# A selective scan re-tiled: eight channels by sixteen states on the partitions, sums in column quadrants, delta spread by DMA

## The chip, the cores and the metric

The kernel runs on one core of a Trainium2 chip. The metric is the device time in microseconds (us) of one execution. Times named below come from the timed runs or from one profiled execution of the kernel before.

## The reference, cut to what matters

A two-layer decoder works on 64 sequences of 128 tokens with 128 features. Layer 0 is a cumulative-sum attention, a cross-attention, and a mixture of experts (two shared ones and eight routed ones, of which each token uses two). Layer 1 is a selective scan, a second cross-attention and a quantised feed-forward part; each of these six blocks ends in a residual and a layer norm. The change is in layer 1's scan and in where the experts of layer 0 are run. The scan has 256 channels `e` and 16 states `n`:

```python
def step(h, inp):
    d_t, u_t, b_t, c_t = inp
    dA = jnp.exp(d_t[..., None] * A)                      # (b, e, n)
    h = dA * h + (d_t * u_t)[..., None] * b_t[:, None, :]
    y = jnp.einsum('ben,bn->be', h, c_t)                  # sum over the states
    return (h, y)
# delta = softplus(dt @ dt_proj_w + dt_bias), A = -exp(A_log); y + u * D follows
```

The experts of layer 0, over the tokens `xf`:

```python
acc = acc + cw[:, None] * ((silu(xf @ e1.T) * (xf @ e3.T)) @ e2.T)   # for 8 routed experts; 2 shared ones have no cw
```

## The kernel before, in words

**Groups.** The 64 sequences are worked in 16 groups `g` of four (`G`), so a row of 512 elements (`W`) holds four sequences of 128 tokens. All is float32 but for the last feed-forward part.

**Order.** Generators (`scan_inputs`, `spread`, `decays`, `states`, `outputs`, `attend`, `feed`, `c_experts` and others) yield steps with an engine, a cost, the keys they depend on and the buffer slots they take. `Flow.run` plays them: it always takes the step with the earliest planned start, shifted by the step's and the thread's `ahead`; a group may start only if it is within `depth` of the oldest unfinished one. A transfer is planned at 0.1 us of the queue and 4.0 us until it lands (`LANDING`). The order that comes out is fixed: each engine then runs its instructions one after the other and waits on semaphores. All transfers are issued on SP's queue.

**Two stages.** Layer 0 runs the first two blocks for all groups, and the experts of the first `EARLY` = 8 groups with weights that stay in memory (`wall`). Layer 1 runs everything else: the experts of the other eight groups with weights streamed in (`streamed`, tile `we`, 384 KB each, ten per group), and the scan, the second cross-attention and the feed-forward part of all groups. An expert group is the lines L302 to L420: hidden products L367, SiLU L384, gate L393, back projection L405, weighting L420.

**The scan.** Channels lie on the partitions, 128 at a time (`c` = 0, 1), and a step `(c, n)` handles two states, so a group has 16 steps and every tile of a step is 128 x 1024. `scan_inputs` computes delta, du = delta * u and the projection that holds B and C; it writes the projection's 48 rows to DRAM (`rows`, L1071). `spread` reads for each step two rows of B and two of C back, broadcast to all 128 partitions (L1154, 512 KB each). `decays` makes dA = exp(A * delta) on ACT, 127 of each 128 tokens, the first being zeroed once so that the scan restarts (L1169). `states` multiplies du with B into PSUM (`bu`, L1185) and runs the scan along the free axis (`h`, L1193), both on DVE. `outputs` multiplies by C on POOL (L1217); that product is held behind the next step's L1185. TensorE then adds the states of the step to `acc` with an identity matrix as weights (L1230):

```python
def add(acc):
    for j in range(2):
        mm(acc, ident, HS[g, c, n][:, j, :], start=n + j == 0, stop=n + j == NS - 1)
```

After the 16 states, L1241 adds u * D. A float32 matmul shows as two records on TensorE, each with its weight load. Other lines that the text names: L825, layer 0's attention-weighted values, 32 output columns per head group; L1475, the output projection of the second cross-attention; L1068, an eviction of the projection; `mid`, the activations that pass from layer 0 to layer 1 through DRAM.

Of the kernel before, what the change touches and what calls it, by code (L numbers as in the profile page):

```python
# [9 lines left out]
BF16 = mybir.dt.bfloat16  # L10
# [6 lines left out]
P = 128  # L17
B = 64
# [11 lines left out]
EARLY = 8  # L30
# [145 lines left out]
def decoder(ctx: ExitStack, tc: tile.TileContext, t: dict, out: bass.AP):  # L176
# [58 lines left out]
    A_log = reserve("A_log", [P, 2, NS])  # L235
# [221 lines left out]
    with (  # L457
# [404 lines left out]
        def resident(g, e):  # L862
# [6 lines left out]
            behind=lambda g: [("lnA", max(0, 2 * g - 2 + 1), 0)] + ([("c", g - 1, "p", 9, 1)] if g else []),  # L869
# [6 lines left out]
        for g in range(EARLY):  # L876
            flow.add(2 * g, c_route(g, S), c_experts(g, S))
# [8 lines left out]
    with (  # L886
# [7 lines left out]
        negA = new(pc, [P, 2, NS], "negA")  # L894
        act(negA, A_log, AF.Exp)
        dve.tensor_scalar(negA, negA, -1.0, None, ALU.mult)

# [14 lines left out]
        missing = new(p, [3, 3, 256], "B0")  # L912
# [17 lines left out]
        for c in range(8):  # L930
            bvb = new(p, [P, P], f"xq{c % 2}")
            dve.tensor_copy(bvb, ybv[:, c : c + 1].to_broadcast([P, P]))
            mm(pbo, bvb, yWo[:, c, :], start=False, stop=c == 7)
# [39 lines left out]
        sl_xT = slots(2, p, [P, W], "xT")  # L973
# [3 lines left out]
        sl_rows = slots(2, pd, [3 * NS, W], "rows")  # L977
        sl_delta = slots(2, p, [P, 2, W], "delta")
        sl_du = slots(2, p, [P, 2, W], "du")
        sl_B = slots(2, p, [P, 2, W], "B")  # L980
        sl_C = slots(2, p, [P, 2, W], "C")
        sl_dA = Slots([new(p, [P, 2, G, P], f"dA{i}") for i in range(3)])
# [13 lines left out]
        sl_xqb = slots(1, p, [P, G, P], "xqb", BF16)  # L996
# [4 lines left out]


        for dA in sl_dA:
            pool.memset(dA.tile[:, :, :, 0:1], 0.0)

# [9 lines left out]
        def scan_inputs(g):  # L1015
# [45 lines left out]
            def project(pj, _):  # L1061
# [8 lines left out]
            (rows_bc,) = yield SP(  # L1070
                k + ("rows",), [k + ("proj",)], lambda o: nc.sync.dma_start(out=o, in_=proj.tile[0 : 3 * NS, :]), sl_rows  # L1071
            )
            rows_bc.until = ("C", g, 1, NS - 2)

# [19 lines left out]
            proj.until = [k + ("dt", 1), k + ("rows",)]  # L1094
            e.until = k + ("e1",)
            delta.until = ("dA", g, 1, NS - 2)
            e = e.tile
            yield ACT(1.1, k + ("exp",), [], lambda: act(e, e, AF.Exp, scale=-1.0), table="exp")
            du.until = ("B", g, 1, NS - 2)
# [9 lines left out]
            yield POOL(2.0, k + ("du",), [], lambda: pool.tensor_tensor(e1, delta.tile, u.tile, ALU.mult), port=True)  # L1109
            IN[g] = u.tile, delta.tile, e1, rows_bc.tile  # L1110
# [30 lines left out]
        def last(g, kind):  # L1141
            return [(kind, g - 1, 1, NS - 2)] if g else []
# [3 lines left out]
        def spread(g):  # L1146

            yield Wait([("in", g, "rows"), ("in", g, "du")] + last(g, "Cin"))
            for c, n in steps:
                for name, sl, row in (("B", sl_B, NS + n), ("C", sl_C, 2 * NS + n)):  # L1150

                    def fetch(o):
                        src = IN[g][3][row : row + 2, :].rearrange("n s -> (n s)").unsqueeze(0)
                        nc.sync.dma_start(  # L1154
                            out=o.rearrange("p n s -> p (n s)"), in_=src.to_broadcast([P, 2 * W])
                        )

                    (o,) = yield SP((name + "in", g, c, n), [("in", g, "rows"), ("in", g, "du")], fetch, sl)
                    o.until = (name, g, c, n)
                    BC[name, g, c, n] = o.tile  # L1160

        def decays(g):
            yield Wait([("in", g, "du")] + last(g, "dA"))
            delta = IN[g][1].rearrange("p c (b s) -> p c b s", b=G)
            for c, n in steps:

                def exps(dA):
                    for j in range(2):
                        act(  # L1169
                            dA[:, j, :, 1:], delta[:, c, :, 1:], AF.Exp, scale=negA[:, c, n + j : n + j + 1]  # L1170
                        )

                (dA,) = yield ACT(1.4, ("dA", g, c, n), [("in", g, "delta")], exps, sl_dA, table="exp")
                dA.until = ("S", g, c, n)
                DA[g, c, n] = dA.tile
# [3 lines left out]
        def states(g):  # L1179
            yield Wait([("in", g, "du")] + last(g, "S"))  # L1180
            for c, n in steps:

                def first(bu):
                    du = IN[g][2]
                    order[g, c, n] = dve.tensor_tensor(  # L1185
                        bu, du[:, c, :].unsqueeze(1).to_broadcast([P, 2, W]), BC["B", g, c, n], ALU.mult
                    )

                (bu,) = yield DVE(1.25, ("B", g, c, n), [("Bin", g, c, n), ("in", g, "du")], first, sl_bu, ahead=AHEAD, port=True)
                bu.until = ("S", g, c, n)  # L1190

                def scan(h):
                    dve.tensor_tensor_scan(  # L1193
                        h.rearrange("p n s -> p (n s)"), DA[g, c, n].rearrange("p n b s -> p (n b s)"),
                        bu.tile.rearrange("p n s -> p (n s)"), 0.0, ALU.mult, ALU.add,
                    )

                (h,) = yield DVE(2.3, ("S", g, c, n), [("dA", g, c, n)], scan, sl_h, ahead=AHEAD)
                h.until = ("acc", g, c, n)
                HS[g, c, n] = h.tile  # L1200
# [7 lines left out]
        def outputs(g):  # L1208
            yield Wait([("in", g, "du")])
            acc = None  # L1210
            for i, (c, n) in enumerate(steps):
# [3 lines left out]
                def product():  # L1215
                    h = HS[g, c, n]
                    one = pool.tensor_tensor(h, h, BC["C", g, c, n], ALU.mult)  # L1217


                    if behind:  # L1220
                        tc.add_manual_dep(one.ins, order[behind].ins.name, BEHIND, reason="shared reads")

                deps = [("S", g, c, n), ("Cin", g, c, n)]
# [3 lines left out]

                def add(acc):
                    for j in range(2):
                        mm(acc, ident, HS[g, c, n][:, j, :], start=n + j == 0, stop=n + j == NS - 1)  # L1230

                if n == 0:
                    (acc,) = yield PE(1.9, ("acc", g, c, n), [("C", g, c, n)], add, sl_acc)
                    acc.until = ("D", g, c)
                else:
                    yield PE(1.9, ("acc", g, c, n), [("C", g, c, n)], lambda: add(acc.tile))
# [275 lines left out]
        def feed(g):  # L1512
# [17 lines left out]
            def rounded(xq):  # L1530
# [8 lines left out]
                lambda o: dve.tensor_scalar(o.rearrange("p b s -> p (b s)"), xq.tile, MAGIC, None, ALU.subtract), sl_xqb,  # L1539
# [90 lines left out]
        def spaced(g):  # L1630

            at = 2 * (g - EARLY)
            return ([("S", at - 1, 1, 0)] if at else []) + ([("c", g - 1, "mix", 9)] if g > EARLY else [])

# [4 lines left out]
        for g in range(EARLY, NG):  # L1639
            flow.add(min(2 * (g - EARLY), g - 1), c_route(g, S), c_experts(g, S))  # L1640
        for g in range(NG):
            flow.add(g, scan_inputs(g), ahead=0.0)
            flow.add(g, gates(g), residual(g), ahead=0.0)
            flow.add(g, spread(g), decays(g), states(g), ahead=-0.5)
            flow.add(g, outputs(g), ahead=0.0)
            flow.add(g, cross_inputs(g), values(g), ahead=-0.5)
            flow.add(g, *(attend(g, b) for b in range(G)), cross_end(g), ahead=0.0)
            flow.add(g, feed(g), ahead=0.0)
        with tc.manual_schedule():
            flow.run(5)  # L1650


def _laid_out(i):
# [18 lines left out]
    def experts(shared, routed, f):  # L1672
# [37 lines left out]
        "A_log": chunks(i[s + "A_log"]),  # L1710
# [35 lines left out]
```

## Time and profile before

| | |
|---|---|
| time, median of 3 runs | 3479.39 us (3478.55 to 3480.17) |
| profiled execution | 3482.17 us, span 3480.5 us, mean granted clock 0.951 |
| layer 0 ends, first scan product, last scan product (start) | 1044, 1111, 3328 us |
| state sum on TensorE, L1230 | 1024 records, 514.4 us |
| moved by DMA | 353.28 MB, mean 102 GB/s |
| B and C broadcasts | 256 + 256 transfers of 512 KB, 4.8 and 4.0 us from issue to landing |
| expert weights streamed, `we` | 80 transfers of 384 KB, 4.4 us |

A line of the groups reads: source line, engine, operation, output tile <- input tiles, shapes, count | busy us in all, mean ns of one | idle time of the engine just before, and what ended it. PE is TensorE's matmul side, PEld its weight loads, DVE is VectorE, ACT ScalarE, POOL GpSimd, SP the engine that issues transfers. Stretches are given in us from the start of the span.

### The profile page before, as it was taken

What the parts mean: (1) busy time and instruction counts of PE and PEld (TensorE: products, weight loads), DVE (VectorE), ACT (ScalarE), POOL (GpSimd) and SP (SyncE); (2) the same over time, 40 slices, a digit from 0 to 9 for tenths busy, and PEclk for the clock granted to TensorE, in tenths of its full rate; (3) what the DMA queues carried; (4) which work ended last, traced back from release to release, by engine and by line L of the source; (5) the groups of instructions that cost most, each with busy time, mean ns of one, the idle gap of its engine ahead of it and who ended that gap; (6) DMA issues with size and microseconds to landing.
All of it is one profiled execution on the core that took longest, in us unless ns stands there. A gap on an engine that the chain in (4) does not pass through costs nothing.

```text
span 3480.5 us, 56211 instructions
## 1 busy us (share of the span) xinstructions
PE 3136.8 (90%) x20760; PEld 2040.5 (59%) x20760; DVE 2731.1 (78%) x5398; ACT 2182.1 (63%) x3739; POOL 1481.3 (43%) x1222
## 2 busy tenths in 40 slices
PE   4999999999987799989988989989998998999974
PEld 2776766766664465645655556656566555566643
DVE  5867787778754788888789888978879888987963
ACT  3656556665544576766666766767676676767743
POOL 4423433433211554544544454355364544534431
PEclk8999999999998899999999999999999999999976
DMA  2001010010004545354333643433434452442310
GB/s 88 25 7 30 24 27 11 24 30 19 10 10 155 180 150 184 128 179 151 127 116 114 205 142 119 145 136 133 156 132 135 141 173 97 154 166 75 107 46 7
DMA packets 141994, 353.28 MB, mean 102 GB/s; under 512 B 31483, under 2 KB 53654, under 8 KB 141590
## 3 DMA queue, kind: packets, MB, share of 16 engines
q1 hardware_dynamic: 141718, 349.68, 30.2%
q8 instruction: 163, 2.67, 0.3%
q14 instruction: 113, 0.93, 0.1%
HBM read 335.47 MB, written 14.16 MB: 100 GB/s over the span
## 4 chain that ended last, share of the span: by engine, by line
PE 61%; DVE 16%; POOL 6%; DMA 5%; ACT 4%; issue 3%; SPq 0%; DVEq 0%; POOLq 0%; ACTq 0%
PE mm L367 13%; PE acc L1230 7%; PE mm L405 7%; POOL h L1217 3%; DVE h L1193 3%; PE mm L802 3%; PE mm L825 3%; PE mm L1040 3%; PE mm L1446 3%; PE mm L1426 3%; PE mm L1376 2%; DMA we<-in_we 2%; DVE bu L1185 2%; PE mm L1475 2%; PE mm L759 2%
## 5 line engine op out<-in xcount | busy, mean ns | idle before, releaser
L1217 POOL TENSOR_TENSOR h<-h,C 128x1024 f32<-128x1024 f32 x256 | 610.3, 2384 | 709.2 <-DVE bu L1185 410.8
L1193 DVE TENSOR_TENSOR_SCAN h<-dA,bu 128x1024 f32<-128x1024 f32 x256 | 584.5, 2283 | 47.6 <-PE acc L1230 29.4
L1230 PE MATMUL acc<-h,ident 128*128 128x512 f32 x1024 | 514.4, 628 | 72.5 <-POOL h L1217 71.9
L1169 ACT ACTIVATE dA<-delta,negA 128x508 f32<-128x508 f32 x512 | 335.4, 713 | 60.3 <-DVE h L1193 52.7
L1185 DVE TENSOR_TENSOR bu<-du,B 128x1024 f32<-128x1024 f32 x256 | 334.0, 1305 | 27.7 <-DMA B<-rows 25.7
L1230 PEld LDWEIGHTS acc<-h,ident 128*128 128x128 f32 x1024 | 186.0, 197 | 287.4 <-issue 159.3
L367 PE MATMUL mm<-cT,we 128*128 128x512 f32 x640 | 315.1, 611 | 29.7 <-DMA we<-in_we 24.0
L367 PE MATMUL mm<-cT,wall 128*128 128x512 f32 x640 | 303.3, 598 | 0.0
L1419 POOL TENSOR_TENSOR s<-s,rs 128x1232 f32<-128x1232 f32 x64 | 148.6, 2321 | 246.5 <-DVE rs L1413 173.2
L785 POOL TENSOR_TENSOR s<-s,mx 128x1232 f32<-128x1232 f32 x64 | 143.9, 2248 | 215.9 <-DVE mx L782 181.3
L384 ACT ACTIVATE a<-mm 128x512 f32<-128x512 f32 x160 | 94.2, 597 | 179.0 <-PE mm L367 169.4
L367 PEld LDWEIGHTS mm<-cT,we 128*128 128x128 f32 x640 | 114.9, 193 | 151.2 <-issue 100.4
L793 ACT COPY pT<-mm 77x512 f32<-77x512 f32 x256 | 133.5, 585 | 84.8 <-PE mm L802 73.2
L1319 PE MATMUL mm<-xT,w_yWq 128*128 128x256 f32 x512 | 169.2, 414 | 12.3 <-ACT kT L1312 6.9
L1437 ACT COPY pT<-mm 77x512 f32<-77x512 f32 x256 | 135.4, 583 | 68.9 <-PE mm L1426 68.0
L405 PEld LDWEIGHTS mm<-wall,eh 128*128 128x128 f32 x1280 | 155.4, 193 | 32.8 <-issue 20.0
L367 PEld LDWEIGHTS mm<-cT,wall 128*128 128x128 f32 x640 | 112.4, 191 | 97.0 <-issue 78.3
L405 PEld LDWEIGHTS mm<-we,ch 128*128 128x128 f32 x1280 | 152.7, 192 | 24.2 <-issue 19.0
L1376 PEld LDWEIGHTS mm<-kT,qT 64*128 64x128 f32 x2048 | 133.7, 196 | 53.9 <-issue 13.9
L1308 ACT ACTIVATE qT<-mm,w_ybq 128x256 f32<-128x256 f32 x256 | 122.2, 477 | 68.2 <-PE mm L1320 66.9
L405 PE MATMUL mm<-wall,eh 128*128 128x128 f32 x1280 | 159.8, 278 | 2.7 <-DVE eh L393 2.7
L1376 PE MATMUL mm<-kT,qT 64*128 64x77 f32 x2048 | 150.8, 287 | 8.6 <-ACT kT L1312 3.8
(313 smaller groups left out, 7160.5 us busy)
## 6 DMA issues: line engine op xcount, KB each, us to landing
B<-rows SPq DMA_DIRECT2D x256, 512.0 KB, 4.8
C<-rows SPq DMA_DIRECT2D x256, 512.0 KB, 4.0
we<-in_we SPq DMA_DIRECT2D x80, 384.0 KB, 4.4
cg<-in_ctxT SPq DMA_DIRECT2D x32, 154.0 KB, 3.5
x<-in_x SPq DMA_DIRECT2D x16, 256.0 KB, 3.8
mid<-x SPq DMA_DIRECT2D x16, 256.0 KB, 2.0
cx<-mid SPq DMA_DIRECT2D x16, 256.0 KB, 5.1
mid<-cx SPq DMA_DIRECT2D x16, 256.0 KB, 2.1
```

What stands on the lines that cost most here:

```text
L367: mm(o, we[e][:, n * 256 + c * P : n * 256 + (c + 1) * P], xT, start=True, stop=True)
L405: mm(py[:, b * P : (b + 1) * P], hf[:, j % 2, b * P : (b + 1) * P], we[f][:, 512 + (j % 2) * P : 512 + (j % 2 + 1) * P], start=j == 0, sto ...
L785: lambda: pool.tensor_tensor(s, s, mx.tile.unsqueeze(2).to_broadcast([P, NH, M]), ALU.subtract), port=True,
L1169: act(dA[:, j, :, 1:], delta[:, c, :, 1:], AF.Exp, scale=negA[:, c, n + j : n + j + 1])
L1185: order[g, c, n] = dve.tensor_tensor(bu, du[:, c, :].unsqueeze(1).to_broadcast([P, 2, W]), BC["B", g, c, n], ALU.mult)
L1193: dve.tensor_tensor_scan(h.rearrange("p n s -> p (n s)"), DA[g, c, n].rearrange("p n b s -> p (n b s)"), bu.tile.rearrange("p n s -> p (n ...
L1217: one = pool.tensor_tensor(h, h, BC["C", g, c, n], ALU.mult)
L1230: mm(acc, ident, HS[g, c, n][:, j, :], start=n + j == 0, stop=n + j == NS - 1)
L1319: mm(pk[:, 0 : 2 * P], yWq[:, cs], xT.tile[:, pair * 2 * P : (pair + 1) * 2 * P], start=True, stop=True)
L1376: mm(sc[:, i * M : (i + 1) * M], qT[r, i, b2 * P : (b2 + 1) * P], kT[r, i, b2 * M : (b2 + 1) * M], start=True, stop=True,)
L1419: lambda: pool.tensor_tensor(s, s, rs.tile.unsqueeze(2).to_broadcast([P, NH, M]), ALU.mult), port=True,
L1437: lambda: nc.scalar.copy(pT[q].rearrange("m i s -> m (i s)"), pt.tile[0:M, :]),
```

## The change

**Scan tiles.** A tile now has eight channels with their 16 states on the 128 partitions: partition 16 r + n is channel r of the tile and state n. A group has 32 such tiles of 512 tokens; a step takes two of them, so steps, shapes and counts on ACT, DVE and POOL stay. The channel of tile `(c, j, m)` is 128 c + 32 j + 8 m + r.

**Delta and du.** They are now what differs by channel, so they are written to DRAM (two transfers of 512 KB per group) and read back by `spread`, each row broadcast to 16 partitions: for every two steps a tile D (delta) and a tile U (du), 128 x 4 x 512 elements each, and each filled by eight transfers of 128 KB into 16 partitions. There are two slots for D and two for U. The exponentials work in place in D.

**B and C.** They are the same for all channels, so one tile of each per group is made by a matmul with a 0/1 matrix (`unfold`) and an eviction on ACT; their broadcasts are gone, and `rows` with them.

**The sum.** `fold` holds for each m a 128 x 32 matrix that sums the states of eight channels into rows 8 m to 8 m + 7. After two steps, four matmuls write the four 32-row quadrants of `acc`; four such rounds (m) make up 128 channels. A tile `h` is kept until the round is done.

**Experts.** `EARLY` is 4: layer 0 runs four groups' experts, spread over its 16 groups, and layer 1 twelve. Planner constants of layer 1 change with it: the spacing of the expert groups, the `ahead` of `gates`, `residual` and `cross_inputs`, and the depth from 5 to 6. `xT` has one slot instead of two, and the quantised rows share the `hb` slot.

The diff, cut to its core:

```diff
-EARLY = 8
+EARLY = 4
...
+        fold = new(pc, [P, 4, 32], "fold")
+        pool.memset(fold, 0.0)
+        for m in range(4):
+            dve.tensor_reduce(
+                fold[:, m, 8 * m : 8 * m + 8], ident.rearrange("p (r n) -> p r n", n=NS), AX.X, ALU.add
+            )
...
-        sl_dA = Slots([new(p, [P, 2, G, P], f"dA{i}") for i in range(3)])
+        sl_dA = slots(2, p, [P, 4, W], "dA")
+        sl_du8 = slots(2, p, [P, 4, W], "du8_")
...
+            for i, v in enumerate((delta.tile, e1)):
+                (d,) = yield SP(
+                    k + ("out", i), [k + ("du",)],
+                    lambda o: nc.sync.dma_start(out=o.rearrange("c p t -> p c t"), in_=v), sl_out[i],
+                )
...
+                def unfolded(o, *_):
+                    mm(o, unfold[i], proj.tile[0 : 3 * NS, :], start=True, stop=True)
...
-            for c, n in steps:
-                for name, sl, row in (("B", sl_B, NS + n), ("C", sl_C, 2 * NS + n)):
+            for c, n in steps[::2]:
+                for i, (name, sl) in enumerate((("D", sl_dA), ("U", sl_du8))):
                     def fetch(o):
-                        src = IN[g][3][row : row + 2, :].rearrange("n s -> (n s)").unsqueeze(0)
-                        nc.sync.dma_start(
-                            out=o.rearrange("p n s -> p (n s)"), in_=src.to_broadcast([P, 2 * W])
-                        )
+                        for r in range(8):
+                            src = IN[g, i][c].rearrange("(j m r) t -> m r j t", j=4, m=4)[n // 4, r]
+                            nc.sync.dma_start(
+                                out=o[NS * r : NS * r + NS], in_=src.unsqueeze(0).to_broadcast([NS, 4, W])
+                            )
+                    o.until = ("S" if i == 0 else "B", g, c, n + 2)
...
-                        act(
-                            dA[:, j, :, 1:], delta[:, c, :, 1:], AF.Exp, scale=negA[:, c, n + j : n + j + 1]
-                        )
+                        act(dA[:, j, :, 1:], dA[:, j, :, 1:], AF.Exp, scale=negA[:, at + j : at + j + 1])
...
-                        bu, du[:, c, :].unsqueeze(1).to_broadcast([P, 2, W]), BC["B", g, c, n], ALU.mult
+                        bu, BC["U", g, c, n], BC["B", g].unsqueeze(1).to_broadcast([P, 2, W]), ALU.mult
...
-                h.until = ("acc", g, c, n)
+                h.until = ("acc", g, c, n | 2)
...
-                    one = pool.tensor_tensor(h, h, BC["C", g, c, n], ALU.mult)
+                    one = pool.tensor_tensor(h, h, BC["C", g].unsqueeze(1).to_broadcast([P, 2, W]), ALU.mult)
...
-                    for j in range(2):
-                        mm(acc, ident, HS[g, c, n][:, j, :], start=n + j == 0, stop=n + j == NS - 1)
+                    for j in range(4):
+                        mm(
+                            acc[32 * j : 32 * j + 32, :], fold[:, m, :], HS[g, c, n - 2 + j // 2 * 2][:, j % 2, :],
+                            start=m == 0, stop=m == 3,
+                        )
...
-            at = 2 * (g - EARLY)
+            at = int(1.25 * (g - EARLY))
...
-            flow.run(5)
+            flow.run(6)
```

## The prediction

> **What bounds the kernel now.** I read the page's engine sums first, then the busy time by stretch, the costliest groups, the chain, and last the transfers.
>
> ```profile
> PE 3136.8 (90%) x20760; PEld 2040.5 (59%) x20760; DVE 2731.1 (78%) x5398; ACT 2182.1 (63%) x3739; POOL 1481.3 (43%) x1222
> ```
>
> TensorE (PE) is the fullest engine. The stretches (length; busy of PE, PEld, DVE, ACT, POOL; granted clock, DMA share, GB/s) show where:
>
> ```profile
> 0.00:1044.00 1044.00, 976.81 (x8612) 682.20 (x8612) 774.17 (x2079) 592.61 (x1062) 353.64 (x481) 0.98 0.09 26
> 1044.00:1111.00 67.00, 51.78 (x171) 28.73 (x172) 23.45 (x60) 23.95 (x32) 8.00 (x8) 0.78 0.42 137
> 1111.00:3330.50 2219.50, 2025.24 (x11398) 1270.39 (x11396) 1863.80 (x3059) 1503.43 (x2522) 1084.52 (x692) 0.96 0.42 143
> 3330.50:3480.50 150.00, 83.00 (x580) 59.22 (x580) 69.68 (x202) 62.07 (x125) 35.17 (x42) 0.70 0.02 6
> ```
>
> Layer 0 (to 1044) is PE's: 94% busy, 99% away from its ends. In the scan stretch (1111 to 3330.5) PE is 91% busy and DVE 84%: two nearly equal limits. The scan's groups there:
>
> ```profile
> L1217 POOL TENSOR_TENSOR h<-h,C 128x1024 f32<-128x1024 f32 x256 | 610.3, 2384 | 709.2 <-DVE bu L1185 410.8
> L1193 DVE TENSOR_TENSOR_SCAN h<-dA,bu 128x1024 f32<-128x1024 f32 x256 | 584.5, 2283 | 47.6 <-PE acc L1230 29.4
> L1230 PE MATMUL acc<-h,ident 128*128 128x512 f32 x1024 | 514.4, 628 | 72.5 <-POOL h L1217 71.9
> L1169 ACT ACTIVATE dA<-delta,negA 128x508 f32<-128x508 f32 x512 | 335.4, 713 | 60.3 <-DVE h L1193 52.7
> L1185 DVE TENSOR_TENSOR bu<-du,B 128x1024 f32<-128x1024 f32 x256 | 334.0, 1305 | 27.7 <-DMA B<-rows 25.7
> ```
>
> The state sum L1230 is PE's largest group. From the chain (start, duration), four of its records take 1.72 us, 0.43 us each, and sixteen records of 128 columns 1.79, 0.112 each:
>
> ```profile
> 1978.18 1.72 PE acc L1230 x4
> ...
> 1983.26 1.79 PE mm L1475 x16
> ```
>
> Layer 0 already sums in 32-column quadrants. In the timeline the first 32 records of 128 columns occupy 502.37 to 503.26:
>
> ```profile
> 502.37 1.08 PE L825 MATMUL mm<-pT,vb 77*32 77x128 f32 x32
> 503.26 1.06 PE L825 MATMUL mm<-pT,one 77*32 77x128 f32 x32
> ```
>
> That is 0.028 us a record, a fourth of 0.112. Last, two stretches holding one transfer each, 96 KB out of 48 partitions (rows, issued 1086.82) and 256 KB out of 128 (mid, issued 1426.30):
>
> ```profile
> 1087.64:1088.42 0.78, 0.78 (x3) 0.29 (x2) 0.21 (x1) 0.23 (x1) 0.00 (x0) 1.00 0.49 126
> ...
> 1427.10:1427.96 0.86, 0.86 (x3) 0.38 (x4) 0.86 (x1) 0.86 (x4) 0.00 (x0) 1.00 0.87 314
> ```
>
> The narrow one ran at 126 GB/s, the wide one at 314.
>
> **What the Trainium skill says.** "TensorE: Matmul & The Clock Gate", Part 3 (packing small matmuls): outputs in distinct 32-partition groups run concurrently; 2.38x for three tiles. L825 shows 4.0x for four; the trace decides. "SBUF — State Buffer", Door 1 (the DMA port swizzle): partitions 0..15 reach 4 of 16 ports, about 109 GB/s (27.2 a port), 128 reach all; the pair above agrees in direction. The same page, "Can I just issue two DMAs to hit both halves?": two at partitions 0 and 64 gained only 6% together. No run here shows eight.
>
> **The change, part by part.**
>
> *State sum.* Per two steps (four states) PE ran 8 records in series: 2 x 1.72 = 3.44 us. Now four 32-column matmuls, still 8 records of 512 columns, four at once: 3.44/4 = 0.86. Over 128 pairs: 440 to 110, minus 330 us. No row has quadrants at 512 columns; bounds are 0 saved (no overlap) and 330; I take 330, since L825 is the same type and quadrant order. New: unfold, 32 matmuls of two records, 64 x 0.43 = 28 us of PE, and 32 evictions at L1068's length, near 0.58, 19 us of ACT, which is 68% busy.
>
> *Experts moved.* Four groups leave layer 0. For eight, layer 0 shows PE 303.3 (L367) + 159.8 (L405) + 13 (router, transposes) = 476, so 238 for four; DVE 106.8 (L393) + 71.4 (L420) + 49 (ranks, norm) = 227, so 114. PE sets layer 0, so it ends at 1044 - 238 = 806; DVE then has 660 in it, 82%, and covers nothing new. Bounds 800 to 850. Layer 1 gains the 238, the 114, and 40 weight loads of 384 KB.
>
> *Scan steps.* Product, scan and POOL product keep shape and count (L1185, L1193, L1217): nothing. The exponentials work in place, same 512: nothing. POOL gains a small memset per group, at most the 0.73 us of L913's larger one, 12 us in all, beside 709 us of its own waiting at L1217. DVE products now wait for eight transfers, not one: 128 x 7 further semaphore waits of 0.02 us (the median of those at L1185), 18 us.
>
> *Buffers.* h is held until the second step's sum, with three tiles and a POOL product between: 0 to about 1 us per pair. DVE would wait and the attention's softmax behind it; I take 0, since the sum itself is quicker.
>
> *Transfers.* Out go B and C, 512 of 512 KB. In come D (delta) and U (du): per pair 16 of 128 KB, each into 16 partitions, 2048 in all, the same 268 MB; plus 32 writes of 512 KB. SP issues one per 0.41 us (L1154's spacing in the timeline), so 16 x 0.41 = 6.6 us a pair. A D transfer holds SP until the scan two tiles back ends; behind it queue U, expert weights, x and mid. Everything but D and U is near 87 MB (120 weight loads 47, out-writes 17, activations 23); at the 350 GB/s that the same view shows for B and C loads (1203.9 to 1204.8), 250 us.
>
> D and U are the unknown. Bounds: 109 GB/s (four ports at a time) is 1.2 us a transfer; SP's 0.41 us is the floor. Successive transfers go to other partitions and eight may be in flight (each waits for the one eight back), so engines that come out of step use different ports. I take midway between 109 and its double, 163 GB/s: 0.80 us each, 1640 us, with the 250 together 1890, inside a scan stretch near 2300. So hidden, though only just. The price is lateness: from a freed D tile to a landed U tile it takes 16 x 0.80 + 2 = 14.9 us. In the changed DVE order, at the durations of before, between those points lies 16.4 us of DVE work in the median, less than 14.9 for 42% of tiles; the shortfalls sum to 120-190 us. Behind a late product stand DVE's softmax and norm steps, and behind those ACT and PE. DVE's idle 12% absorbs most; I add 30 (bounds 0 and 190).
>
> *Sum.* DVE in the scan stretch: 1864 + 114 + 18 = 1996; PE: 2025 - 330 + 28 + 238 = 1961. They are level, and neither can fill to 99%. With DVE at 87.5%, between its 84% and PE's 91% of before: 2281, plus 30: 2311. With 806 ahead, 67 + 10 of start (the first D and U tiles come late), and 150 at the end: 3344. The profiled execution took 1.7 us beyond its span (3482.17 against 3480.5) and lies 2.8 above the median of 3479.39; I say **3345**.
>
> **The rivals.** (1) *As summed*, 3235 to 3440: DVE at 92% gives 3235, at 84% 3441. For it: the L825 rows, and DVE's 47.6 us of waiting at L1193 in 2219.
>
> (2) *Partition-bound transfers, slower.* If the engines stay in step, each transfer takes 1.2 us: 2048 x 1.2 = 2460, + 250 = 2710 for the stretch, which every engine then waits for: 806 + 77 + 2710 + 150 + 2 = 3745; with the skill's 6% overlap 3605. For it: the narrow transfer's 126 GB/s and the skill. Against: eight in flight, not two. It turns slower than before when the stretch passes 2447, that is (2447 - 250)/2048 = 1.07 us a transfer, 122 GB/s.
>
> (3) *In between*: 122 to 140 GB/s, or lateness paid in full and more: 3440 to 3600. This holds the 0.2% band, about 7 us, the least that a measurement of this kernel tells from no change.
>
> (4) *Quadrants do not overlap at 512 columns*: PE keeps 2291 in the stretch, at 91% 2510: 3545.
>
> **How the numbers follow.** (1) 0.53, (2) 0.28, (3) 0.15 (0.09 faster, 0.03 the same, 0.03 slower), (4) 0.04. Faster 0.62, same 0.03, slower 0.35. Both signs have weight: the likeliest case alone is 3235 to 3440; the range, leaving out the end of (1) and the upper part of (2), is 3230 to 3700.
>
> **What would show it.** Right: layer 0 ends near 806; the fold matmuls take 0.86 us per eight records; DVE above 85% in the scan stretch, few waits of bu on DMA; D and U tiles land 7 to 9 us after their first issue. Wrong: DMA busy above 90% of the stretch with under 125 GB/s, and bu and dA waiting on DMA by hundreds of us (2); fold records 0.43 us apart (4); layer 0 past 850.

## The result, and the profile after

The changed kernel takes 4332.07 us (4325.64 to 4343.0, four runs) against 3478.97 (3470.95 to 3480.17) for the kernel before in the same comparison: a ratio of 1.2462, 95% interval 1.2427 to 1.2496. It is 853 us slower where 134 us faster was forecast, and it lies above the range (3230 to 3700). The profiled execution has a span of 4341.0 us.

The engine sums of the page of the kernel after:

```profile
PE 3179.4 (73%) x20824; PEld 2039.7 (47%) x20824; DVE 2744.9 (63%) x5404; ACT 2197.0 (51%) x3773; POOL 1464.3 (34%) x1236
```

No engine has noticeably more to do than before (DVE 2731.1, ACT 2182.1, POOL 1481.3); all of them stand still more. The busy time by stretch of the same kernel: layer 0, the start of layer 1, the scan stretch, and the end (columns as in the prediction: length; busy of PE, PEld, DVE, ACT, POOL; granted clock, DMA share, GB/s):

```profile
0.00:889.00 889.00, 780.12 (x7604) 557.20 (x7604) 662.91 (x1779) 521.74 (x945) 347.73 (x465) 0.95 0.09 27
889.00:991.00 102.00, 61.62 (x189) 31.81 (x190) 27.62 (x70) 24.71 (x35) 8.24 (x7) 0.73 0.58 124
991.00:4187.50 3196.50, 2248.39 (x12373) 1382.57 (x12372) 1983.30 (x3343) 1582.22 (x2660) 1072.98 (x722) 0.81 0.71 108
4187.50:4341.00 153.50, 89.31 (x661) 68.16 (x660) 71.11 (x213) 68.30 (x135) 35.32 (x43) 0.73 0.02 6
```

The loss is in the third line (the second adds 35 us against before). The scan stretch is 3196.5 us, not 2311. DVE's work in it is what was forecast (1983 against 1996), but that is 62% of the stretch, and PE is at 70%. The DMA engines are 71% busy at 108 GB/s: neither full nor idle, which is the riddle of this case.

The scan's groups on the page of the kernel after, with the experts' hidden products:

```profile
L1249 POOL TENSOR_TENSOR h<-h,C 128x1024 f32<-128x1024 f32 x256 | 604.9, 2363 | 1422.3 <-DVE bu L1215 1205.9
L367 PE MATMUL mm<-cT,we 128*128 128x512 f32 x960 | 578.8, 732 | 524.8 <-DMA we<-in_we 488.6
L1225 DVE TENSOR_TENSOR_SCAN h<-dA,bu 128x1024 f32<-128x1024 f32 x256 | 584.3, 2282 | 48.1 <-PE acc L1267 30.3
L1204 ACT ACTIVATE dA<-dA,negA 128x508 f32<-128x508 f32 x512 | 329.8, 707 | 343.1 <-DMA du<-du 179.9
L1215 DVE TENSOR_TENSOR bu<-du,B 128x1024 f32<-128x1024 f32 x256 | 336.1, 1313 | 245.8 <-DMA du<-du 109.2
L1267 PE MATMUL acc<-h,fold 128*32 128x512 f32 x1024 | 186.8, 678 | 64.7 <-POOL h L1249 64.6
```

The durations hold: scan 2282 ns, product 1313, POOL's product 2363. The state sum L1267 did what was expected of it, 186.8 us in place of 514.4, and waiting for it at L1225 stayed at 30.3 us (29.4 before). New is who ends the idle time: transfers, in front of PE (L367), ACT (L1204) and DVE (L1215). The quadrants overlap at 512 columns as well; in the timeline of the kernel after (start, duration) eight records take 1.06 us, where four took 1.72 before and 0.86 was forecast for eight:

```profile
2418.13 1.06 PE L1267 MATMUL acc<-h,fold 128*32 128x512 f32 x8
```

SP's queue, the waits of the kernel after (engine, line, waited for: us in all, times, longest us):

```profile
SPq L1187 <- DMA dA<-delta: 551.6, 885, 1.9
SPq L1187 <- DVE h L1225: 507.4, 76, 32.6
SPq L1667 <- PE mm L405: 453.5, 42, 22.6
...
SPq L1187 <- DMA du<-du: 159.6, 260, 1.6
```

The first and the last are short waits of a transfer for the one eight places back: there the transfers set the pace. The second and third are long: there the queue stands, because the D buffer it wants is still being scanned, or because an expert weight in it waits for PE. From the issue times of D and U in the trace: 1483 us of their 3192 us are spent in bursts, with issues at most 2 us apart, and 1709 us lie in 119 longer pauses. In a burst the first eight go out about 0.47 us apart, and from the ninth on the median is 0.97. That answers the riddle: over the bursts the DMA engines' share is 1.00, over the pauses 0.48. The two tiles issued from 2422.39 on, in a stretch of the kernel after:

```profile
2422.40:2437.90 15.50, 7.86 (x12) 3.25 (x13) 2.52 (x3) 1.49 (x3) 2.00 (x1) 0.57 1.07 149
```

What a pause and the catching up after it look like, in the timeline of the kernel after:

```profile
2419.32 2.29 DVE L1225 TENSOR_TENSOR_SCAN h<-dA,bu 128x1024 f32<-128x1024 f32 x1 [0.44 <-PE acc L1267]
2421.39 0.35 SPq L1667 DMA_DIRECT2D we<-in_we  x1
2422.39 7.83 SPq L1187 DMA_DIRECT2D dA<-delta  x8
...
2430.04 6.42 PE L367 MATMUL mm<-cT,we 128*128 128x512 f32 x8 [10.84 <-DMA we<-in_we]
2430.93 6.97 SPq L1187 DMA_DIRECT2D du<-du  x8
...
2433.90 0.69 DVE L393 TENSOR_TENSOR ch<-fh,mm 128x512 f32<-128x512 f32 x1 [12.29 <-PE mm L367]
...
2434.50 1.23 DVE L1215 TENSOR_TENSOR bu<-du,B 128x1024 f32<-128x1024 f32 x1
```

The expert weights go out at 2421.39 and share the way with tiles: PE gets them at 2430.04. PE's products feed DVE's L393, which waits 12.29 us; the next scan product stands behind L393 in DVE's order and starts at 2434.50, though nothing shows it waiting for its own data. POOL, behind DVE, waits too. The engines wait for a queue that issues one thing after another, and it in turn waits for them.

### The profile page after: what moved, and what is told of

The parts are those of the page before. It is cut to its first block, busy times and chain, and to the rows that moved or that the text cites. A ratio compares the mean times of both kernels' runs of the same rounds, so it can differ in the third digit from the quotient of the medians.

```text
span 4341.0 us, 58372 instructions
## 1 busy us (share of the span) xinstructions
PE 3179.4 (73%) x20824; PEld 2039.7 (47%) x20824; DVE 2744.9 (63%) x5404; ACT 2197.0 (51%) x3773; POOL 1464.3 (34%) x1236
## 5 line engine op out<-in xcount | busy, mean ns | idle before, releaser
L367 PE MATMUL mm<-cT,we 128*128 128x512 f32 x960 | 578.8, 732 | 524.8 <-DMA we<-in_we 488.6
L1225 DVE TENSOR_TENSOR_SCAN h<-dA,bu 128x1024 f32<-128x1024 f32 x256 | 584.3, 2282 | 48.1 <-PE acc L1267 30.3
L367 PEld LDWEIGHTS mm<-cT,we 128*128 128x128 f32 x960 | 197.5, 228 | 757.2 <-issue 541.5
L1204 ACT ACTIVATE dA<-dA,negA 128x508 f32<-128x508 f32 x512 | 329.8, 707 | 343.1 <-DMA du<-du 179.9
L1215 DVE TENSOR_TENSOR bu<-du,B 128x1024 f32<-128x1024 f32 x256 | 336.1, 1313 | 245.8 <-DMA du<-du 109.2
L384 ACT ACTIVATE fh<-mm 128x512 f32<-128x512 f32 x240 | 141.3, 596 | 545.3 <-PE mm L367 537.9
L393 DVE TENSOR_TENSOR ch<-fh,mm 128x512 f32<-128x512 f32 x240 | 160.9, 680 | 388.7 <-PE mm L367 310.7
L405 PEld LDWEIGHTS mm<-we,ch 128*128 128x128 f32 x1920 | 254.8, 211 | 63.6 <-issue 39.1
L405 PE MATMUL mm<-we,ch 128*128 128x128 f32 x1920 | 261.3, 295 | 8.1 <-DVE ch L393 4.1
L1267 PE MATMUL acc<-h,fold 128*32 128x512 f32 x1024 | 186.8, 678 | 64.7 <-POOL h L1249 64.6
L785 POOL TENSOR_TENSOR s<-s,mx 128x1232 f32<-128x1232 f32 x64 | 143.8, 2248 | 199.8 <-DVE mx L782 140.6
L1467 PE MATMUL mm<-ident,s 128*77 128x128 f32 x1024 | 154.0, 303 | 44.4 <-ACT pT L1478 26.0
L420 DVE SCALAR_TENSOR_TENSOR cx<-mm,ccw,cx 128x128 f32<-128x128 f32 x384 | 107.5, 343 | 121.5 <-PE mm L405 119.6
L1467 PEld LDWEIGHTS mm<-ident,s 128*77 128x77 f32 x1024 | 130.5, 165 | 74.8 <-ACT pT L1478 31.1
L1439 DVE TENSOR_REDUCE mx<-mm 128x4 f32<-128x308 f32 x256 | 119.5, 467 | 71.3 <-PE mm L1417 71.3
```

The costliest lines, as they stand in the source:

```text
L367: mm(o, we[e][:, n * 256 + c * P : n * 256 + (c + 1) * P], xT, start=True, stop=True)
L393: lambda: dve.tensor_tensor(h[:, c, :], a.tile, p3.tile, ALU.mult),
L405: mm(py[:, b * P : (b + 1) * P], hf[:, j % 2, b * P : (b + 1) * P], we[f][:, 512 + (j % 2) * P : 512 + (j % 2 + 1) * P], start=j == 0, sto ...
L1204: act(dA[:, j, :, 1:], dA[:, j, :, 1:], AF.Exp, scale=negA[:, at + j : at + j + 1])
L1215: order[g, c, n] = dve.tensor_tensor(bu, BC["U", g, c, n], BC["B", g].unsqueeze(1).to_broadcast([P, 2, W]), ALU.mult)
L1225: dve.tensor_tensor_scan(h.rearrange("p n s -> p (n s)"), BC["D", g, c, n].rearrange("p n s -> p (n s)"), bu.tile.rearrange("p n s -> p (n ...
```

## The experiments

The kernel before ran beside every group of runs, at 3473.5 to 3482.6 us. The first four runs ask which half of the change loses the time and what a transfer costs; the letters in their expectations are of an earlier set. From f1 on, **P** is the theory that the transfers' own time makes the stretch long, and **Q** that the fixed order of work, planned as if a tile cost SP's queue 0.1 us, makes queue and engines wait for one another.

### The two halves of the change

The new scan with eight groups' experts in layer 1, as before the change (the planner constants of layer 1 as before too):

```diff
-EARLY = 4
+EARLY = 8
```

> The new scan alone: experts of eight groups back in layer 0, planner constants as before the change. Theory Q (the D and U transfers are slow, about 1.0 us each, and SP's queue with them holds up whatever stands behind): still slow, 3900 to 4400 us; layer 0 ends near 1044, the D and U interval inside a burst stays at 1.0 us, and the expert weights still wait for DMA, a third less often. Theory X (the four further groups' experts overload layer 1): below 3550 us.

Measured: 4230.95 us, 1.2156 (1.2104 to 1.2208), 101 less than the changed kernel. And the reverse, the scan of the kernel before with the twelve groups of the change (and its planner constants):

```diff
-EARLY = 8
+EARLY = 4
```

> The scan of before with twelve groups' experts in layer 1 and the new planner constants. Theory Q: near before, 3350 to 3550 us, PE waiting little for expert weights (under 80 us in all). Theory X: above 3800 us, PE waiting hundreds of us for expert weights.

Measured: 3597.21 us, 1.0335 (1.0299 to 1.0372), so 115 us: more than the band expected, and far from the 853. The loss sits in the scan's half. The experts cost 100 to 115 us with either scan, where the prediction gave them a gain.

### What a transfer costs

A kernel of transfers alone, with rows and destinations as in `spread`, and variants of them (the first of them, and the one over every eighth partition). In the expectations, the *ports* theory says that the time depends on the partitions that a transfer reaches, the *count* theory that it does not:

```python
nc.sync.dma_start(out=tiles[k % 4][NS * r : NS * r + NS], in_=row(k, r))
nc.sync.dma_start(out=tiles[k % 4].rearrange("(n r) j t -> r n j t", r=8)[r], in_=row(k, r))
```

> Transfers alone, 16 MB of reads in each of seven stretches, nothing else computed (the output holds copied data). Ports theory: into 16 neighbouring partitions 0.9 to 1.2 us per 128 KB; every eighth partition 0.6; quarter-blocks issued in the order 0 4 1 5 2 6 3 7 about as neighbours; 128 partitions 512 KB in 1.3 to 1.7 us (0.4 per 128 KB); 16 neighbours with 8 KB rows as with 2 KB rows; 32 neighbours 256 KB in 1.2 to 1.4 us; from two queues as from one. Count theory: every 128 KB transfer 0.9 to 1.1 us whatever the partitions.

Its page, the GB/s in 40 slices of the span:

```profile
GB/s 122 131 131 131 131 138 138 138 204 214 207 201 206 180 167 167 167 167 166 228 410 410 261 184 189 185 187 184 216 224 224 223 186 185 186 189 188 177 132 293
```

In order: 16 neighbouring partitions per transfer, as in the change, 131 to 138 GB/s, or 0.983 us per 128 KB from the mean distance of the issues; every eighth partition, 201 to 214 (0.640 us); neighbours in the order 0 4 1 5 2 6 3 7, 167 (0.786); 128 partitions, 410 (0.32 per 128 KB); 16 neighbours with rows of 8 KB in place of 2, 184 to 189 (0.706); 32 neighbours, 256 KB each, 216 to 224 (1.18 us); 16 neighbours issued in turn by SP's and ACT's queues, 177 to 189. It is one execution. The count theory is out, and the ports theory is not the whole either: it expected the other order, the longer rows and the second queue to change nothing. The 0.983 us agrees with the 0.97 in the kernel's bursts. The estimate in the prediction was 0.80.

So the same scan with partition p = 8 n + r in place of 16 r + n, which lays each transfer over the whole height (`fold`, `unfold` and the layout of A_log change to match):

```diff
-                                out=o[NS * r : NS * r + NS], in_=src...
+                                out=o.rearrange("(n r) j t -> r n j t", r=8)[r], in_=src...
```

> The changed kernel with channel and state swapped on the partitions (8 n + r instead of 16 r + n), so that each of the same 2048 transfers of 128 KB goes to every eighth partition instead of 16 neighbours. Ports theory: [...]the interval in a burst falls from 1.0 to about 0.6 us and the time to 3500 to 3900 us. Count theory (number of transfers, eight in flight, completion latency): interval and time as in the changed kernel, 1.0 us and 4330 us.

Measured: 3881.52 us, 1.1152 (1.1114 to 1.1191), with 0.638 us between issues. So it is not the count of transfers that sets the time; a third less per transfer took off 451 us, more than half of the loss. The trace also shows what sets the new pace. The issues of the kernel after and of this run (duration on SP's queue in ns: least, median, most):

```profile
L1187 SPq DMA_DIRECT2D du<-du x1024: 302/303/1804, 955.5 to 4144.1; - x171
```

```profile
L1187 SPq DMA_DIRECT2D du<-du x1024: 532/593/1635, 959.3 to 3686.0; - x171
```

A strided transfer holds the queue for 593 ns while it is issued (532 at the least; why is not shown), nearly the whole 638 from issue to issue, and the waits for the one eight places back, 885 and 260 of them in the kernel after, are all but gone (9). The queue, no longer the data, is what a burst waits for. And yet 99 pauses of over 2 us still add up to 1450 us. Next, a tile in one transfer of 1 MB to 128 partitions (each gets another channel's row, so the state values differ from the reference's):

```diff
-                        for r in range(8): ...
+                        nc.sync.dma_start(out=o, in_=IN[g, i][c].unsqueeze(1).to_broadcast([P, 4, W]))
```

> Each D or U tile is filled by one transfer of 1 MB to 128 partitions (every partition gets its own channel's row four times), in place of eight to 16 neighbours each; the bytes per tile and all waits stay, the data spread is another, so the state values are not the reference's. At the measured 410 GB/s a tile takes 2.6 us in place of 8.0. Theory P (the transfers' own time makes the layer long; the strided run gave 451 us for 737 us of transfer time less): 3350 to 3550 us. Theory Q (waits of the in-order queue, whatever a tile takes): 3750 to 4100 us.

Measured: 3568.15 us, 1.0267 (1.0235 to 1.0299), just above the band of P. Up to here P looks right: the cheaper the transfer, the faster the kernel.

### What the plan knows of it

The changed kernel with one number of the planner changed. The instructions, the buffers and the transfers are the same; only the order differs:

```diff
-                    (o,) = yield SP((name + "in", g, c, n), ..., fetch, sl)
+                    (o,) = yield SP((name + "in", g, c, n), ..., fetch, sl, cost=8.0)
```

> The changed kernel with nothing but the planner's price of a D or U tile changed: 8.0 us on SP's queue, as measured, in place of 0.1; so another order of the same instructions. Theory Q (the order, planned as if transfers cost nothing, makes SP's queue, PE and DVE wait in turn): 3700 to 4100 us. Theory P (the transfers' own time): 4250 to 4400 us, as before the edit.

Measured: 3666.13 us, 1.0549 (1.0509 to 1.0589): **666 us less, with the slow transfers kept.** It is better than Q's band. Its scan stretch:

```profile
978.50:3543.30 2564.80, 2100.59 (x12454) 1296.73 (x12476) 2008.56 (x3419) 1617.20 (x2701) 1093.47 (x738) 0.90 0.86 136
```

The same work now fills 2565 us, and the DMA share went from 71 to 86% at 136 GB/s, the rate that the transfers alone reached. The pauses fell from 1709 to 1094 us, and the queue's wait for PE, with a weight at its head, from 453.5 to 134.8. PE's wait for weights shrank, the waits after and in this run:

```profile
PE mm L367 <- DMA we<-in_we: 488.6, 65, 30.2
```

```profile
PE mm L367 <- DMA we<-in_we: 116.9, 31, 11.6
```

One changed order can be luck. If it is the rate that counts, too low and too high a price, 4.0 and 12.0, must both cost time:

```diff
-                    ..., fetch, sl, cost=8.0)
+                    ..., fetch, sl, cost=4.0)
```

> The changed kernel with the planner's price of a D or U tile at 4.0 us, half of what was measured. If what helps is that the plan spreads the tiles at the rate at which the ports bring them: the plan still puts too many into a stretch, 3800 to 4150 us. If the price only shook the order into a luckier one: anything, as likely near 3670 as near 4330.

> The changed kernel with the planner's price of a D or U tile at 12.0 us, half as much again as measured. If spreading at the right rate is what helps: the plan leaves the ports idle part of the time and its scan stretch is nearer to 256 x 12 = 3070 us than to 2560, so 3700 to 4250 us. If any high price does: 3640 to 3700 us.

Measured, both as expected if the rate counts: 3903.09 us at 4.0 (1.124, 1.1174 to 1.1305) and 4236.92 at 12.0 (1.2201, 1.2132 to 1.227). With 4332 at 0.1 and 3666 at 8.0 the time has its lowest of the four where the price is the measured one (8 x 0.98 = 7.9 us). The scan stretches at 4.0 and at 12.0:

```profile
976.00:3751.00 2775.00, 2181.35 (x12419) 1347.01 (x12436) 1990.82 (x3349) 1615.72 (x2687) 1082.45 (x728) 0.87 0.80 126
```

```profile
976.00:4102.60 3126.60, 2194.74 (x12446) 1308.29 (x12469) 2006.52 (x3416) 1598.03 (x2675) 1082.82 (x735) 0.81 0.70 112
```

At 12.0 the stretch is close to the 256 x 12 = 3072 us that the plan allots, and the DMA share is down to 0.70 with PE's wait for weights as short as in f2 (120.3 us): the too dear plan leaves the transfers idle. At 4.0 that wait is 249.6 us: the too cheap plan asks for data sooner than it comes. Is it enough to tell the plan that a tile comes late?

```diff
-                    (o,) = yield SP((name + "in", g, c, n), ..., fetch, sl)
+                    (o,) = yield SP((name + "in", g, c, n), ..., fetch, sl, landing=12.0)
```

> The changed kernel; the planner is told that a D or U tile lands 12 us after its issue in place of 4, but not that it holds the queue (0.1 us, as in the change). If what hurt was that each tile came late: 3650 to 3800 us, as with the price of 8.0. If what hurt was that the plan put more tiles into a stretch than the ports can bring, and none into the next: 4100 to 4350 us.

Measured: 4270.01 us, 1.2287 (1.223 to 1.2344). No: lateness told brings 62 us, occupancy told 666. Last, the weights issued by ScalarE's queue:

```diff
-            (w,) = yield SP(("we", g, e), [], lambda o: nc.sync.dma_start(...), sl_we)
+            (w,) = yield SP(("we", g, e), [], lambda o: nc.scalar.dma_start(...), sl_we)
```

> The changed kernel, with the experts' weight loads of layer 1 issued by ScalarE's queue in place of SP's, at the same places of the order. If SP's queue stops mainly because a weight load in it waits for PE, and PE for a weight load that stands behind D and U tiles (453 and 489 us of such waits): 3850 to 4100 us. If the queue is stopped by the tiles' own two buffers and by the ports: 4250 to 4400 us, the weight waits of PE going over to other engines.

Measured: 4250.14 us, 1.2229 (1.2194 to 1.2264), the lower edge of the second case. PE's wait for weights fell from 488.6 to 178.5 us, the time by only 82. But SP's queue did not get free of the weights. Where it had waited 453.5 us to issue them, its tiles now wait about as long for the weights that ACT's queue has issued, since the transfer some eight places back can be one of those:

```profile
SPq L1187 <- DMA we<-in_we: 441.1, 72, 12.2
```

So this run does not break the circle, and how much of the loss the weights carry stays open.

### What the new scan is worth once it is fed

Price and layout, each with eight and with twelve groups (the runs with eight have the planner constants of layer 1 as before too). The edits are those above, put together; h3 keeps `EARLY` at 4, and the price is 5.1 for the strided form (f3, h3), 8.0 for neighbours (g3) and 2.6 for the one transfer of 1 MB (g2):

```diff
-EARLY = 4
+EARLY = 8
-                    ..., fetch, sl)
+                    ..., fetch, sl, cost=5.1)
```

> Three edits together: each transfer to every eighth partition (0.64 us each measured), the planner's price of a tile 5.1 us, and eight groups' experts in layer 0 as before the change. If the three add up: the strided run's 3882, less the 101 us that the experts gave, less what the order gives. Theory Q: 3450 to 3700 us. Theory P: 3750 to 3850 us.

> The changed kernel's transfers to 16 neighbours, the planner's price of a tile 8.0 us, and eight groups' experts in layer 1 as before the change. The experts gave 101 us in the unpriced order and 115 in the kernel before: 3550 to 3580 us if the parts add up, and then the strided form gives nothing once the order is right. If the ports' 2050 us now bind: 3640 to 3680 us, no better than with twelve groups.

> The strided transfers with the planner's price of 5.1 us and twelve groups' experts in layer 1, the one cell not yet run beside 3666 (neighbours, twelve), 3777 (neighbours, eight) and 3605 (strided, eight). If the strided form lifts the ports' limit, twelve groups cost as in the kernel before: 3680 to 3720 us. If ports or the ring of eight still bind, twelve groups fill waits and are no worse: 3560 to 3610 us.

> One 1-MB transfer to 128 partitions for a tile (another spread of the data than the reference's), the planner's price of a tile 2.6 us, and eight groups' experts in layer 1 as before the change: what the new scan could give if its data came nearly free. If transfers still hold the strided, priced run (3605): 3380 to 3480 us. If they no longer do, and DVE's, PE's and ScalarE's order holds it: 3520 to 3610 us.

Measured: 3604.89 us (1.0375, 1.0354 to 1.0396), 3777.25 (1.0862, 1.0822 to 1.0903), 3510.22 (1.0108, 1.0051 to 1.0165) and 3469.23 (0.9981, 0.9968 to 0.9993). The runs of the new scan by layout, plan and groups, us:

| a tile's transfers | plan at 0.1 us, 12 groups | plan at 0.1, 8 | plan at the measured time, 12 | the same, 8 |
|---|---|---|---|---|
| 16 neighbours, 7.9 us | 4332 | 4231 | 3666 | 3777 |
| every eighth partition, 5.1 us | 3882 | | 3510 | 3605 |
| one of 1 MB, 2.6 us | 3568 | | | 3469 |

With the plan right, twelve groups are *better* than eight, by 111 and by 95 us; with the plan wrong, or with the old scan, they are worse by 101 and 115. For the neighbours that is g3's second case, and further out than its band. It would fit that the transfers need their 2050 us in layer 1 whatever else is there, so that work taken out of it only lengthens layer 0. For the strided form, 3510 lies below both of h3's bands: twelve groups fill waits there too. And g2 in its first band says that the strided transfers still held f3 by 136 us. The scan stretch of this kernel, and that of the one with 1-MB transfers and eight groups:

```profile
968.50:3367.00 2398.50, 2086.56 (x12420) 1288.59 (x12436) 1984.81 (x3359) 1580.64 (x2665) 1090.35 (x735) 0.92 0.48 145
```

```profile
1123.00:3344.00 2221.00, 1863.24 (x11453) 1156.63 (x11477) 1916.19 (x3116) 1507.60 (x2554) 1102.54 (x719) 0.90 0.42 148
```

DVE is 83% busy in the first and 86% in the second, as near to the assumed 87.5% as any run came. With eight groups and nearly free data the new scan only equals the kernel before, so PE's 330 us are not on the path by themselves. To see it directly, the strided, priced kernel with eight groups got its state sum back in full width:

```diff
-                            acc[32 * j : 32 * j + 32, :], fold[:, m, :], HS[...][:, j % 2, :],
-                            start=m == 0, stop=m == 3,
+                            acc, ident, HS[...][:, j % 2, :],
+                            start=m == 0 and j == 0, stop=m == 3 and j == 3,
```

> The strided, priced run with eight groups' experts, its state sum done as before the change: each record multiplies by a full 128x128 matrix and its result takes all 128 rows, so that no two run beside each other (about 514 us of PE in place of 187; the planner's price of a step 3.8 in place of 1.0; the sums are of other rows than the reference's). If the quadrants' 330 us are on the path of layer 1: 3850 to 3950 us. If PE's relief lies beside DVE's work and the transfers: 3600 to 3700 us.

Measured: 3663.66 us, 1.0542 (1.0494 to 1.0591), 59 more, the second case. The group of the run with quadrants and of the run without, from their pages:

```profile
L1267 PE MATMUL acc<-h,fold 128*32 128x512 f32 x1024 | 228.4, 715 | 139.9 <-POOL h L1249 139.6
```

```profile
L1267 PE MATMUL acc<-h,ident 128*128 128x512 f32 x1024 | 512.1, 642 | 78.8 <-POOL h L1249 78.7
```

284 us more of PE in that group cost 59 us of time. What the quadrants buy may be room: with the new scan, once its plan is right, twelve groups' experts turn from a loss (e2) into a gain (h3 against f3). A full-width sum with twelve groups, which would show it, wasn't run.

### A version that beats both was not found

Three more attempts from the 3510 us. Rows of 8 KB in DRAM, so that a transfer reads one row per partition and not four, with a price of 4.0:

```diff
+                            src = IN[g, i][c].rearrange("(m r j) t -> m r (j t)", m=4, j=4)[n // 4, r]
```

> The strided, priced kernel with twelve groups, delta and du written to DRAM with the four channels of a partition side by side, so that a transfer reads one row of 8 KB for each of its 16 partitions in place of four of 2 KB (the writes take four transfers in place of one). Among 16 neighbours rows of 8 KB took 0.71 us in place of 0.98, so about 0.46 us is expected here in place of 0.64; the planner's price of a tile is 4.0. If transfers still hold the 3510 us: 3420 to 3480 us. If the engines' own work holds it: 3490 to 3530 us.

Measured: 3570.31 us, 1.0275 (1.0253 to 1.0297): a miss on both sides. The issues stayed 0.632 us apart, so rows of 8 KB don't help a strided transfer: its issue still takes 587 ns of the queue. The price of 4.0 was then too low for 5.1. Price 6.0 on the strided kernel, and, with the price back at 5.1, ten groups (the spacing of the expert groups to match):

```diff
-                    ..., fetch, sl, cost=5.1)
+                    ..., fetch, sl, cost=6.0)
```

```diff
-EARLY = 4
+EARLY = 6
```

> The strided kernel with twelve groups and the planner's price of a tile at 6.0 us in place of 5.1 (256 x 6.0 = 1540 us, still well inside the stretch of 2400). If a little slack in the plan absorbs the transfers' spread: 3440 to 3500 us. If 5.1, the measured value, is the best: 3520 to 3600 us.

> The strided kernel with the price of 5.1 us and ten groups' experts in layer 1 (six in layer 0). If layer 0 can take two more groups at less than its 50 us each in idle PE time: 3460 to 3500 us. If ten lies between twelve (3510) and eight (3605): 3540 to 3570 us.

Measured: 3496.35 us (1.004, 1.0028 to 1.0052) and 3517.66 (1.0102, 1.0079 to 1.0125). The first, at the upper end of its band for some slack, is the lowest of the new scan with its real data, though its ratio's interval still meets h3's, and it is 0.4% behind the kernel before. Ten groups, between their two bands, are as good as twelve. Nearly free data with the right price *and* twelve groups wasn't run; by the 95 us between f3 and h3, an estimate for it is 3469 - 95 = 3374.

## Why the prediction was wrong

**The step that failed is the price of lateness**, "I add 30 (bounds 0 and 190)". It measured the shortfall of each tile against the DVE work that lay before it, added the shortfalls, and took the order as something that absorbs them. The stretch took 885 us more than the 2311 forecast, and f2, with the same transfers in another order, takes 666 us off the kernel, 632 of them in the stretch. Two things were wrong in it. It looked at the delay of a tile, and g4 shows that a plan which knows the delay, and not the rate, gains only 62 us. And it compared the transfers' sum with the whole stretch (1890 in about 2300, "hidden, though only just"), though the order does not use the stretch evenly: inside a group, the kernel before starts a scan every 6.45 us in the median, then turns to other work. The data of one scan step takes 16 x 0.98 / 2 = 7.9 us. In the changed kernel these starts came to 8.61 us in the median and 11.33 in the mean; in f2, whose plan knows the pace, to 7.96 and 9.52. The bound of 190 bounded the wrong quantity.

**The transfer's price was too low**, 0.80 us against 0.98 (the Trainium skill's "SBUF — State Buffer", Door 1, gives 109 GB/s for 16 partitions, from which an estimate is 1.2 us; measured 131 to 138, so part of the hoped-for overlap is there). From f2 to h3, 0.98 to 0.64, it is worth 156 us once the plan is right. The 0.41 us taken as SP's floor was that of another transfer: the strided form is issued in 0.59. By the prediction's own rule the sign would still have been "faster", since it turned only at 1.07 us. So rival (2), which had the right resource, gave neither the mechanism nor the size: its flag, DMA above 90% busy, shows 71%. None of the four rivals was a queue that alternates between bursts and pauses.

**Layer 0 ends at 889, not 806**, outside its bounds of 800 to 850. PE lost 197 us of the 238: the experts' two products L367 and L405 did leave (463 us before, 235 after), but the rest of PE's work took 31 us more, at a granted clock of 0.95 in place of 0.98. And its idle time rose from 67 to 109 us: from 800 to 890 PE is 65% busy, where the last 89 us of layer 0 before had it at 90%. Experts had probably filled the gaps of the last groups. Even the best plans kept this (903 us in h3). The step took a busy engine's work for time.

**The start** took 102 us in place of 77, the end 153.5 in place of 150. Together: 83 + 885 + 25 + 4 = 997 us, the distance of the span, 4341.0, from the 3344 of the forecast's sum.

**What held.** DVE's work in the stretch (1996 said, 1983 found), the quadrants, the unchanged scan steps, and nothing for h's longer hold; unfold took 43.2 us where 28 were said. That the state sum saved 328 us where 330 were forecast is partly luck: the group was put at 440 us and 110, and was 514 and 187. PE's work did not hold, 1961 said and 2248 found; in h3 it is 2087. Part of it goes with the lower granted clock (below): L367's 960 records alone, 121 ns longer each, make about 116 us. (In rival (4), 2291 us at 91% is 2518, not 2510.) The assumed 87.5% for DVE was reached nearly, by runs that had their data. From h3's 3510 to the forecast of 3345, 165 us remain: 97 in layer 0, 88 in the stretch, less 19 at start and end.

**What stays open.** Which waits of the order, one by one, make up the 666 us was not taken apart: a new price reorders everything. That the rate is the cause rests on the four prices and on g4, and each price is one order. Not tried: more than two slots for D and for U, though the queue waits 507 us for a D buffer still being scanned and 482 in f2; and tiles issued by two queues, which was faster in the transfers alone.

## What to carry to other kernels

If a fixed order is planned with costs, every new resource that the change loads must have its cost in the plan: a transfer queue that holds a step's data for 7.9 us, planned at 0.1, cost more here than the slow transfers themselves. Compare what a queue can bring with the pace *inside a burst*, not with the mean over a stretch. And spread each transfer over distant partitions before counting on several in flight, and then look at what the issue itself costs the queue.

## What the runs showed of the hardware that was not expected

Eight transfers in flight to 16 neighbouring partitions each ran at 131 to 138 GB/s together. Another issue order alone gave 167, two queues in turn 177 to 189, rows of 8 KB 184 to 189, every eighth partition 201 to 214, 128 partitions 410. The strided form stayed at 0.63 to 0.64 us per transfer with rows of 2 KB and of 8 KB, because issuing one held SP's queue for 593 and 587 ns, where neighbours took 303. In the transfers alone the DMA share was then 0.83, against 1.07 for neighbours (the shares of this view can pass 1; the columns are length, POOL, granted clock, DMA share, GB/s):

```profile
0.00:120.00 120.00, 0.20 (x4) 1.00 1.07 132
130.00:195.00 65.00, 0.00 (x0) 1.00 0.83 209
```

TensorE's granted clock was lower where PE was less busy: 0.96 in the scan stretch of the kernel before (PE 91% busy), 0.92 in h3 (87%), 0.90 in f2 (82%), 0.81 in the changed kernel (70%). Which of the two drives the other was not tested. The same experts' matmul L367 with streamed weights takes 611, 664, 664 and 732 ns in these four. So PE's total went up, from 3136.8 to 3179.4 us, although its largest group had lost 328 us; and in g1 a group longer by 284 us lengthened PE's busy time in the stretch by only 192 (1909 to 2101), at a clock of 0.93 in place of 0.88.
